# A drain at the end of each TensorE step in a graph-network layer, with the waits of the step's users moved to it

## The chip, the core and the metric

The kernel runs on one core of one Trainium2 chip. The metric is the device time of one execution in microseconds (us), the median of several runs. The engines are called as in the profile: PE (TensorE; PEld its weight loads), DVE (VectorE), ACT (ScalarE), POOL (GpSimd) and SP (SyncE). A "q" behind a name (PEq, PEldq, POOLq) means the engine's sequencer, the part that takes instructions from the queue, waits on semaphores and hands the work to the engine.

## The reference

One layer of a graph network, with 12,500 nodes of 64 numbers and 212,500 edges of 32 numbers. The edges come sorted by their destination. All data is float32.

```python
msg_in = jnp.concatenate([nodes[row], nodes[col], edge_features], axis=-1)
messages = relu(msg_in @ mW1 + mb1) @ mW2 + mb2
aggregated = jax.ops.segment_sum(messages, col, num_segments=12500)
upd_in = jnp.concatenate([nodes, aggregated], axis=-1)
out = layernorm(nodes + relu(upd_in @ uW1 + ub1) @ uW2 + ub2)
```

Here `row` is the source (`src`) and `col` the destination (`dst`) of each edge.

## The kernel before

The kernel has two branches; these inputs run `ordered`, which uses that the edges are sorted. The edges are cut into 554 groups (`G`) of three tiles of 128 edges; the last group has two tiles. All edges of a group go to at most 32 neighbouring nodes (a window, `W`), so that the node part of a message needs only 32 rows.

A group g passes through these parts:

- **gather(g)** (L129, L132): POOL starts three indirect DMAs, one a tile, that fetch the source nodes' rows into `own.s[g % 20]`. They wait for `turn_by[g - 20]`, the TensorE step that turned the group that had this buffer before. The loop calls `gather(k + 16)` after step k.
- **onehot(g)** (L303, L306): DVE writes the one-hot of each edge's destination in the window beside the gathered rows.
- **turn(g)** (L312): PE transposes the three tiles (L318) into PSUM, and ACT copies the result to `own.st` (L326), with a sum on the side that counts the edges of each node.
- **hidden(g)** (L334): six matmul records (three matmuls) give the hidden layer of the messages (L339), with the window's weights `own.wm`, and ACT applies relu (L349).
- **sums(g)** (L359): PE transposes the counts (L363), and three matmuls (six records, L365) add up the hidden rows of each destination. DVE adds the sums to `agg` (L374) and the counts to `xc` (L375).
- **windows(b)** (L288, L292): once in four groups a matmul makes the node part of the weights for the next four groups, and DVE copies it to `own.wm` (L297).
- **update** (L381): once a chunk of 512 nodes has all its edges, the node's own two-layer network, the residual and the layer norm follow, in pieces that `step_update` spreads over several steps. Its tiles (`u_ps`, `u`, `y` and so on) come from pools, and their waits are found from the tiles; they don't hang on the steps.

The order of the work is written out by hand. `step(*work)` (L445) issues the PE part of several parts, one behind the other, and then the ACT and DVE parts that use their results (`follow`). The waits are written by hand too: `after(first, *others)` lets one instruction wait for others. The first PE instruction of a step waits for everything that the step needs. Its other PE instructions wait for nothing, and only the last, `did[-1]`, raises PE's semaphore; the others are taken out of the semaphores by `no_tile_sem_insts`. That last instruction is given to each `follow`, which notes it in `turn_by`, `hidden_by` or `sums_by` and makes its ACT or DVE instruction wait for it. Gathers, one-hots and the loads of `own.st` wait for the steps in these notes as well.

In the main loop step k does turn(k), hidden(k-2) and sums(k-4) together. The PSUM buffers `own.ps` are two, taken in turn, so a step uses what ACT and DVE did for step k-2. The last ten values of k (`SHORT`) are split: a step with turn(k) alone, then up to two steps of sums, then up to two of hidden. `onehot(k + 1)` is called before step k.

## Time and profile before

| what | value |
|---|---|
| median of 3 runs | 2105.08 us (2103.44 to 2107.8) |
| profiled execution, its own time | 2103.22 us |
| its span, first to last instruction | 2101.4 us |
| mean granted clock of TensorE | 0.934 |
| PE busy | 1412.9 us (67%) |
| POOL busy | 1571.9 us (75%) |
| DVE, ACT busy | 575.0 us (27%), 553.4 us (26%) |
| PE 83 to 2049 us, busy | 1334.14 us of 1966 us |
| PE 2049 to 2096 us, busy | 37.03 us of 47 us |

A group row of the profile gives the line, the engine, the operation, what it writes and reads, the count, then the busy time in us and the mean of one in ns, and behind the second bar the time in which the engine sat idle just before these instructions and what ended most of it. In a timeline the columns are the start, the length, the engine, the line and the operation, and in brackets the idle time before it and what ended it. In the chain of waits the columns are start, length and what; "issue" is time in which the engine waited for nothing that the profile shows. In a row of one line or tile the three numbers are the least, median and greatest length in ns, then the first and last start. A releaser is inferred: it is the one that came last by the profile. The ends of matmuls are modelled.

### The profile page before, as it was taken

How to read it: one execution, taken by the hardware profiler on the slowest of the kernel's cores; microseconds unless marked ns; L12 is line 12 of the kernel's file. 1: busy time of each engine (PE TensorE's matmuls, PEld its weight loads, DVE VectorE, ACT ScalarE, POOL GpSimd, SP SyncE). 2: the span in 40 equal slices, each digit the busy share in tenths (PEclk: the TensorE clock that was granted, in tenths of full speed). 3: DMA queues.
4: the chain of work that ended last, by engine and by line, in shares of the span. 5: the costliest groups of instructions: out<-in, count | busy, mean ns of one | idle time of the engine just before them, and what ended most of it. 6: DMA issues, size and time to landing. Idle time of an engine off the chain costs nothing.

```text
span 2101.4 us, 30666 instructions
## 1 busy us (share of the span) xinstructions
PE 1412.9 (67%) x9441; PEld 1202.9 (57%) x9441; DVE 575.0 (27%) x3191; ACT 553.4 (26%) x1715; POOL 1571.9 (75%) x1668
## 2 busy tenths in 40 slices
PE   3766766666766767667666776776666766766667
PEld 2655655555655556556555665565555655655555
DVE  5322232222222223232222222222222223222222
ACT  1322222222222222222222222222222222222222
POOL 7777777777777777777777777777777777777774
PEclk9999999999999998999999999998999999999998
DMA  4321121221212112212121112121212121212211
GB/s 112 82 47 41 45 44 42 43 45 41 47 38 47 43 42 43 45 41 47 39 47 41 44 43 44 41 48 38 47 41 45 44 45 42 46 40 45 43 43 27
DMA packets 73364, 96.05 MB, mean 46 GB/s; under 512 B 33451, under 2 KB 40842, under 8 KB 73194
## 3 DMA queue, kind: packets, MB, share of 16 engines
q0 software_dynamic: 53152, 54.51, 13.8%
q1 hardware_dynamic: 19128, 39.03, 6.8%
q8 instruction: 80, 1.31, 0.3%
q14 instruction: 90, 0.74, 0.1%
q10 hardware_dynamic: 914, 0.46, 0.1%
HBM read 90.58 MB, written 3.20 MB: 45 GB/s over the span
## 4 chain that ended last, share of the span: by engine, by line
PE 40%; DMA 22%; issue 14%; POOL 12%; ACT 6%; DVE 5%; SPq 0%; POOLq 0%; ACTq 0%; DVEq 0%
DMA own_s<-in_x,src_sb 21%; PE own_ps L365 15%; POOL own_s L132 12%; PE own_ps L339 12%; PE own_ps L318 8%; ACT own_h L349 4%; ACT own_st L326 2%; PE own_ps L363 2%; DVE xc L375 1%; DVE own_s L306 1%; PE own_ps L292 1%; PE u_ps L405 1%; DVE agg L374 1%; PE u_ps L392 1%; PE u_ps L393 1%
## 5 line engine op out<-in xcount | busy, mean ns | idle before, releaser
L132 POOL DMA_INDIRECT own_s<-in_x,src_sb x1661 | 1571.1, 946 | 507.2 <-issue 355.3
L318 PE MATMUL own_ps<-own_ident,own_s 128*96 128x128 f32 x1661 | 300.2, 293 | 642.7 <-DVE own_s L306 250.9
L326 ACT ACTIVATE own_st<-own_ps 96x384 f32<-96x384 f32 x554 | 268.8, 485 | 1410.7 <-PE own_ps L365 1019.8
L318 PEld LDWEIGHTS own_ps<-own_ident,own_s 128*96 128x96 f32 x1661 | 171.6, 135 | 739.6 <-ACT own_h L349 691.1
L365 PE MATMUL own_ps<-own_s,own_h 128*128 128x128 f32 x3322 | 567.3, 312 | 0.0
L339 PE MATMUL own_ps<-own_wm,own_st 128*128 128x128 f32 x3322 | 502.7, 292 | 0.6 <-DVE own_wm L297 0.6
L374 DVE TENSOR_TENSOR agg<-own_ps,agg 128x32 f32 x554 | 106.0, 191 | 1397.9 <-ACT own_h L349 1369.0
L365 PEld LDWEIGHTS own_ps<-own_s,own_h 128*128 128x128 f32 x3322 | 454.7, 207 | 24.0
L339 PEld LDWEIGHTS own_ps<-own_wm,own_st 128*128 128x128 f32 x3322 | 455.6, 208 | 2.1 <-DVE own_wm L297 0.8
L349 ACT ACTIVATE own_h<-own_ps 128x384 f32<-128x384 f32 x553 | 262.3, 474 | 17.8 <-PE own_ps L339 17.8
L297 DVE COPY own_wm<-own_ps 32x128 f32<-32x128 f32 x550 | 155.1, 282 | 6.8 <-issue 0.8
L306 DVE TENSOR_TENSOR own_s<-iota,dlc 128x96 f32<-128x96 f32 x554 | 133.0, 241 | 4.3 <-issue 0.2
L363 PE MATMUL own_ps<-own_ident,own_counts 32*1 32x32 f32 x554 | 103.8, 187 | 3.8 <-ACT own_h L349 1.9
L326 ACT ACTIVATION_READ_ACCUMULATOR own_st<-own_ps 96x1 f32 x554 | 105.4, 190 | 0.0
L375 DVE TENSOR_TENSOR xc<-own_ps,xc 1x32 f32 x554 | 99.2, 179 | 14.7 <-PE u_ps L393 12.6
L363 PEld LDWEIGHTS own_ps<-own_ident,own_counts 32*1 32x1 f32 x554 | 41.1, 74 | 78.0 <-issue 13.6
L285 DVE COPY xw<-xc 66x32 f32 x554 | 62.6, 173 | 3.1 <-DMA xc<-in_xT 2.2
L292 PE MATMUL own_ps<-w1b,xw 66*128 66x128 f32 (+1 forms) x276 | 55.7, 284 | 0.0
L405 PE MATMUL u_ps<-u,u 128*128 128x64 f32 (+1 forms) x196 | 48.5, 391 | 0.5 <-ACT u L395 0.5
L405 PEld LDWEIGHTS u_ps<-u,u 128*128 128x128 f32 (+1 forms) x196 | 47.4, 326 | 1.0 <-ACT u L395 0.9
L292 PEld LDWEIGHTS own_ps<-w1b,xw 66*128 66x128 f32 (+1 forms) x276 | 44.2, 201 | 0.1
L407 DVE TENSOR_TENSOR y<-u_ps,xin 128x256 f32<-128x256 f32 (+1 forms) x25 | 10.5, 419 | 78.2 <-PE u_ps L405 78.2
(58 smaller groups left out, 203.6 us busy)
## 6 DMA issues: line engine op xcount, KB each, us to landing
own_s<-in_x,src_sb POOLq DMA_INDIRECT x1661, 2.4
own_st<-in_efT SPq DMA_DIRECT2D x138, 192.0 KB
xin<-in_x SPq DMA_DIRECT2D x24, 128.0 KB
out<-o SPq DMA_DIRECT2D x24, 128.0 KB
xc<-in_xT SPq DMA_DIRECT2D x12, 179.2 KB
dlc_i<-in_dst_cols SPq DMA_DIRECT2D x1, 831.0 KB
xc<-in_xT SPq DMA_DIRECT2D x4, 179.5 KB
src_sb<-in_src SPq DMA_DIRECT2D x13, 50.5 KB
```

Source lines behind the costliest of these rows:

```text
L132: nc.gpsimd.indirect_dma_start(out=s[:p, j, W:], out_offset=None, in_=x[:, :], in_offset=bass.IndirectOffsetOnAxis(ap=src_sb[:p, g * TG + ...
L292: did = nc.tensor.matmul(wp[: n * W, :], xw[:, :n, :], w1b, start=True, stop=True)
L297: c = nc.vector.tensor_copy(wm[g % NW][:W, :], wp[i * W : (i + 1) * W, :])
L306: places_by[g] = nc.vector.tensor_tensor(own.s[g % RING][:, :, :W], iota.unsqueeze(1).to_broadcast([P, TG, W]), dlc[:, g * TG : (g + 1) * ...
L318: nc.tensor.transpose(xt[:, j * P : j * P + p], s[:p, j, :], ident[:p, :p])
L326: nc.scalar.activation(t[: D + W, c : c + n], xt[:, :n], AF.Copy, accum_out=counts[:, g : g + 1]), step)
L339: nc.tensor.matmul(pre[:p, j, :], t[:, c + j * P : c + j * P + p], wm[g % NW], start=True, stop=True)
L349: relu_by[g] = [nc.scalar.activation(h, pre, AF.Relu)]
L363: did = [nc.tensor.transpose(sg[0:1, TIMES, :], counts[:W, g : g + 1], ident[:W, :W])]
L365: did.append(nc.tensor.matmul(sg[:, :TIMES, :], h[:p, j, :], s[:p, j, :W].unsqueeze(1).to_broadcast([p, TIMES, W]), start=j == 0, stop=j = ...
L374: after(nc.vector.tensor_tensor(agg[:, at], sg[:, 0, :], agg[:, at], ALU.add), step),
L375: after(nc.vector.tensor_tensor(xc[0:1, at], sg[0:1, TIMES, :], xc[0:1, at], ALU.add), step),
```

## The change

```diff
@@ -458,7 +458,8 @@
                 for b in [b for b in xws if (b - 1) * SB <= g][:1]:
                     last, copies = windows(b, own.ps[g % 2][:, 2, (TIMES + 1) * W :][:, :H])
                     did.append(last)
-        for i in did[:-1]:
+        did.append(nc.tensor.drain())
+        for i in did[:-2] if copies else did[:-1]:
             tc.no_tile_sem_insts.add(i.ins.name)
             tc.add_to_no_dep_group("quiet", i.ins)
         for part, g, _, _, follow in parts:
```

The pieces of `update` are issued after the step's last instruction, in the loop below the diff (`step_update(g)`), so they stand behind the drain on PE's queue.

## The prediction

> **What bounds the kernel now.** I read the costliest groups first, then the timeline of the gather queue, the chain of waits around one steady step and in the last 50 us, and last the rows by line. PE is busy longest of the compute engines (1412.9 us, 67%), but the row that matters is POOL's:

> ```profile
> L132 POOL DMA_INDIRECT own_s<-in_x,src_sb x1661 | 1571.1, 946 | 507.2 <-issue 355.3
> ```

> 1661 gathers of 946 ns, and most of the idle time before them is put down to "issue", which is no wait. The timeline of POOL, early, in the middle and at the end:

> ```profile
> 6.83 0.94 POOL L132 DMA_INDIRECT own_s<-in_x,src_sb  x1 [0.30 <-issue]
> 8.07 0.94 POOL L132 DMA_INDIRECT own_s<-in_x,src_sb  x1 [0.30 <-issue]
> ...
> 1008.27 0.94 POOL L132 DMA_INDIRECT own_s<-in_x,src_sb  x1 [0.30 <-issue]
> 1009.51 0.94 POOL L132 DMA_INDIRECT own_s<-in_x,src_sb  x1 [0.30 <-DMA own_s<-in_x,src_sb]
> ...
> 2078.95 0.90 POOL L132 DMA_INDIRECT own_s<-in_x,src_sb  x1 [0.30 <-issue]
> ```

> The pitch is 1.25 us throughout, with the same 0.30 us gap whether a releaser is named or not, and also at 7 us, before PE has begun its steps. So POOL never waits: 1661 x 1.25 = 2076 us of the 2101.4 us span, three gathers (3.75 us) a group. What PE waits for is seen in the chain of waits:

> ```profile
> 1008.27 2.50 DMA own_s<-in_x,src_sb
> 1010.77 0.14 issue
> 1010.91 0.51 PE own_ps L318 x3
> ```

> The third gather of a group starts at 1008.27, lands 2.50 us later, and PE's step starts 0.14 us after that. The next groups' third gathers, 1012.01 and 1015.75, give 1014.51 and 1018.25; the steps start at 1014.61 and 1018.43. The trace names a DVE instruction as releaser of those two, because it ended a moment before PE started. But the one-hot that step k needs is queued on DVE ahead of the adds of step k-1 (`onehot(k + 1)` stands before `step`), so it has been done for a step. A step's matmuls take about 2.15 us; in the windows view PE is busy 1334 us of the 1966 us between 83 and 2049 us. Over 1966 / 3.75 = 524 steps that leaves 1.2 us of idle PE a step, waiting for gathers.

> From 2049 us it is different. The last ten groups are split into separate steps, and the chain of waits runs through PE and ACT to the end without a gather in it:

> ```profile
> 2082.80 0.86 PE own_ps L365 x6
> 2083.66 0.68 PE own_ps L339 x6
> 2084.38 0.04 issue
> 2084.43 0.50 ACT own_h L349
> 2084.93 0.04 issue
> 2084.97 0.18 PE own_ps L363
> ```

> A sums step is followed at once by a hidden step, ACT's relu waits for that, the next sums step waits for the relu. Only here, in about 46 us, can a cost at the end of a step reach the end of the kernel.

> **The change part by part.**

> *In the steady part.* 580 drains are added to PE's queue, one a step (544 full steps, then 10 turns, 14 sums, 12 hiddens). Behind each stands the next step's first transpose, and in between its semaphore instructions. All of that lies in PE's 1.2 us of mean idle time, before the next gather has landed, so I cost it at nothing; without that cover it would cost y a step (below), 0.28 x 544 = 152 us. ACT and DVE get the step's end a little later, but step k needs only what they did for step k-2. POOL's gather for k+16 waits for the turn of step k-4, about 20 steps earlier: not late either. The loads on SP's queue wait for a hidden step nine steps before their use. At half clock a step's span grows to 3.73 us (2030.36 to 2034.09), just under POOL's 3.75; a drain puts PE some 0.3 us a step behind there, and it catches up at full clock. Early on (36 to 83 us) PE runs steps back to back, and the drains only stretch that stretch.

> *In the tail*, two prices. y: a step that starts behind another one's last matmul on PE. x: ACT or DVE waiting for a step's end. No row of this trace has a drain behind a busy array, so they are built from near rows:

> ```profile
> L365 PE MATMUL own_ps<-own_s,own_h x3322: 270/275/581, 44.9 to 2090.3; 128*128 128x128 f32 x196
> ...
> L318 PEldq EVENT_SEMAPHORE  x1243: 51/51/3273, 34.1 to 2085.4; - x178
> ...
> L826 PEldq DRAIN  x1: 8/8/8, 0.3 to 0.3; - x1
> ```

> A matmul lasts 0.275 us (median), but six take 0.86 us in the chain, a pitch of 0.143: each overlaps the one before by 0.13 us, and over a step's boundary that overlap goes. The drain itself is 0.008 us on an idle PE. I add 0.04 us for one hop, as "issue" shows between engines in the tail, and 2 x 0.051 us because the next weight load and matmul now come into the queue after the drain (the nearest row for an instruction on PE's sequencer is the 51 ns semaphore one). y = 0.13 + 0.008 + 0.04 + 0.10 = 0.28 us. x = 0.008 + 0.04 = 0.05 us, a second hop.

> Counting in the chain from 2049.04 on: PE goes from one step straight into the next work at 2051.75, 2053.47, inside the hidden pair after it, 2056.62, 2057.60, 2058.58, inside the next pair, 2066.54, 2068.90, 2073.34, 2079.03, 2080.75, 2083.66, 2086.02 and 2088.38, 15 times: 15 x 0.28 = 4.2 us. ACT or DVE takes over from a step's end 11 times (2049.56, 2055.47, 2060.00, 2062.37, 2064.87, 2067.22, 2081.99, 2084.34, 2086.70, 2088.94, 2090.53): 11 x 0.05 = 0.55 us. Besides, in five groups a turn stands between the hidden step and the sums step that waits for the relu. It had 0.30 us to spare (2084.67 to 2084.97). Now it starts y and two semaphore instructions (0.10) later and its own drain and restart (0.15) follow: 0.53 - 0.30 - 0.05 (x, already counted) = 0.18 us over, 5 x 0.18 = 0.9 us. Sum: 4.2 + 0.55 + 0.9 = 5.65 us.

> Bounds: the least is the drain row alone, 15 x 0.008 = 0.1 us. A gain is no end: the drain removes no work and cannot come before the matmul it follows. The most takes POOL's 0.30 us gap between two instructions as the restart: y = 0.43, 15 x 0.43 = 6.5 us, x = 0.15, 1.7 us, the turns 5 x 0.5 = 2.5 us, together 10.7 us. I take the middle, since its rows are PE's own.

> [...]

> **The rivals.**
> *The drain is nearly free.* The matmul's modelled end may lie after its real one, so the drain finds PE quiet at once and the restart hides under it: place, the same 15 crossings; price 0.05 us each, and no turn late: 15 x 0.05 + 0.55 = 1.3 us, 2106.4 us, no difference. It decides from y under about 0.2 us, where the sum falls below 0.2% (4.2 us, about what a measurement of this kernel can tell from no change). For it: the 8 ns row. Against: the 0.13 us overlap is real pitch, not a modelled end.
> *The steady part loses its cover.* If drain and restart took over the 1.2 us of idle, say 1.5 us, PE would be the bound: 0.3 x 544 = 163 us, about 2270 us. For it: no row bounds a drain under load. Against: every PE sequencer row here is 8 or 51 ns.
> *Faster.* Were the sequencer's semaphore earlier than the matmul's by the whole 0.04 us hop, 11 x 0.04 = 0.4 us comes back, 2104.7 us; only the spread of runs (2103.44 to 2107.8) would make more of it.

> **How the numbers follow.** The profiled execution took 2103.22 us (span 2101.4 and 1.8 around it); with the sum, 2108.9. The median of the runs is 1.9 us above the profiled one: 2105.08 + 5.65 = 2110.7 us, +0.27%. Chances: forecast 0.58, nearly free 0.34, lost cover 0.04, faster 0.04. Slower by over 0.2% is 0.58 + 0.04 = 0.62, within 0.34, faster 0.04. The range runs from 2105.0 (the 0.1 us bound) to 2117.0 (2105.08 + 10.7 and 1.2 us of spread); it leaves out the lost cover and the gains.

> **What would show it.** Right: POOL's pitch stays 1.25 us with the 0.30 us gap; steps still start 0.1 to 0.2 us after the third gather's landing; between 50 and 80 us plain steps that now start 1.98 us apart (58.71, 60.70, 62.67) start about 2.3 apart; POOL's last gather is still near 2079 us, and the time from it to the end, 22.5 us now, and from the first split step (2049) grow by 4 to 7 us. Wrong: a POOL pitch over 1.25 us, PE idle under 0.2 us in a steady step, or a granted clock well off 0.934, since a slower TensorE would leave its cover.

## The result and the profile after

The kernel with drains takes 2118.96 us (median of 4 runs, 2116.78 to 2124.34), the kernel before 2104.91 us beside it (4 runs, 2103.44 to 2107.8): a ratio of 1.0074 [1.0061, 1.0086], 14.05 us slower. I had forecast 5.65 us more and a range up to 2117.0. The profiled execution is the longest of the four, 2124.34 us with a span of 2122.5 us, so its tail shows the loss at its largest. Its granted clock is 0.910, where the kernel before has 0.934.

ACT's row in the kernel before:

```profile
L326 ACT ACTIVATE own_st<-own_ps 96x384 f32<-96x384 f32 x554 | 268.8, 485 | 1410.7 <-PE own_ps L365 1019.8
```

Three lines of after that answer to those of before, two groups of the page and the last gather in POOL's timeline:

```profile
L132 POOL DMA_INDIRECT own_s<-in_x,src_sb x1661 | 1572.5, 947 | 507.2 <-issue 370.6
L326 ACT ACTIVATE own_st<-own_ps 96x384 f32<-96x384 f32 x554 | 268.8, 485 | 1380.9 <-PEq L461 1329.8
...
2080.41 0.90 POOL L132 DMA_INDIRECT own_s<-in_x,src_sb  x1 [0.30 <-issue]
```

POOL is unchanged: 947 ns a gather, the same 507.2 us before them. ACT's wait now ends with PE's sequencer at line 461, the drain. The last gather starts 1.46 us later than before (2078.95). From there to the end of the span it takes 42.1 us, where it took 22.45. So 19.65 of the 21.1 us that this execution is longer show behind the last gather, in the split tail.

The row of the drain and one of its waiters, by line:

```profile
L461 PEldq DRAIN  x580: 438/2105/4497, 37.6 to 2110.7; - x194
...
  ACT own_st L326: 1329.8, 499
```

The 438 to 4497 ns contain the wait for the step's matmuls, so they are no price: in after's trace each of the 580 drains ends 0.02 to 0.05 us behind the modelled end of its step's last matmul, and the one of the step at 74.79, for example, starts at 74.86 and lasts 2.105 us, to 76.96. The price is in the gaps of PE. First the early phase, where steps run back to back (PE's timeline):

```profile
74.79 0.51 PE L318 MATMUL own_ps<-own_ident,own_s 128*96 128x128 f32 x3 [0.77 <-ACT own_st L326]
...
77.28 0.51 PE L318 MATMUL own_ps<-own_ident,own_s 128*96 128x128 f32 x3 [0.34 <-issue]
```

Plain steps are 2.49 us apart (1.98 before), with 0.34 us between the modelled end of the last matmul and the next transpose. Now the tail, in the chain of waits:

```profile
2078.03 0.08 issue
2078.11 1.65 PE own_ps L339 x6
2079.76 0.33 issue
2080.09 0.85 PE own_ps L318 x3
2080.94 0.08 issue
2081.02 0.21 PE own_ps L363
```

Into most hidden and sums steps PE loses 0.08 us behind the modelled end; into most turns, whose first instruction has two semaphore waits ahead of it, 0.34 us. Over all stops of after the least gap is 0.08 us with no semaphore instruction between the drain and the next matmul, 0.23 with one, 0.33 with two and 0.45 with three. Besides, the overlap with the matmul before is lost, 0.17 us at the end of a full step in before's timeline. Those are the stops I had priced. What I had not priced is the third column from the right of the windows view (span, busy time and instructions of PE, PEld, DVE, ACT and POOL, then TensorE's granted clock, DMA share, GB/s), first before, then after:

```profile
2050.00:2073.00 23.00, 19.99 (x129) 16.25 (x130) 6.72 (x36) 6.71 (x20) 17.28 (x19) 0.93 0.17 36
2073.00:2082.00 9.00, 7.63 (x34) 6.74 (x35) 4.29 (x22) 1.25 (x4) 5.32 (x6) 0.62 0.18 40
2082.00:2102.00 20.00, 8.91 (x58) 6.80 (x56) 3.34 (x18) 3.82 (x13) 0.00 (x0) 0.75 0.03 9
```

```profile
2050.00:2073.00 23.00, 19.15 (x79) 15.19 (x79) 5.04 (x27) 3.70 (x11) 17.21 (x20) 0.57 0.17 34
2073.00:2082.00 9.00, 8.01 (x32) 5.93 (x31) 1.30 (x7) 2.13 (x6) 6.49 (x7) 0.50 0.16 28
2082.00:2125.00 43.00, 26.23 (x114) 18.51 (x113) 8.55 (x45) 7.17 (x21) 0.00 (x0) 0.70 0.03 9
```

With drains TensorE runs at half clock from about 2053 to 2087 and from 2094 to 2104 us, 44 us in all; before it did so from 2051 to 2054 and from 2075 to 2082, 10 us, apart from the last few matmuls of each. The 1.65 us for six matmuls in the chain above is half clock too; at full clock it is 0.91.

### The profile page after: what moved, and what is told of

Same layout as the page of the kernel before. It is cut to its first block, busy times and chain, and to the rows that moved or that the text cites. A ratio compares the mean times of both kernels' runs of the same rounds, so it can differ in the third digit from the quotient of the medians.

```text
span 2122.5 us, 31419 instructions
## 1 busy us (share of the span) xinstructions
PE 1473.7 (69%) x9441; PEld 1238.3 (58%) x9441; DVE 574.5 (27%) x3191; ACT 554.1 (26%) x1715; POOL 1573.3 (74%) x1668
## 4 chain that ended last, share of the span: by engine, by line
DMA 32%; POOL 23%; PEldq 15%; issue 15%; PE 4%; ACT 4%; PEld 3%; DVE 3%; POOLq 0%; DVEq 0%; ACTq 0%
DMA own_s<-in_x,src_sb 32%; POOL own_s L132 23%; PEldq L461 15%; ACT own_st L326 2%; ACT own_h L349 2%; PEld own_ps L318 1%; PEld own_ps L365 1%; PE own_ps L365 1%; PE u_ps L405 1%; PEld own_ps L339 1%; DVE xc L375 1%; PE own_ps L339 1%; PE u_ps L392 1%; DVE agg L374 0%; PE u_ps L393 0%
## 5 line engine op out<-in xcount | busy, mean ns | idle before, releaser
L132 POOL DMA_INDIRECT own_s<-in_x,src_sb x1661 | 1572.5, 947 | 507.2 <-issue 370.6
L318 PE MATMUL own_ps<-own_ident,own_s 128*96 128x128 f32 x1661 | 301.7, 294 | 594.8 <-DVE own_s L306 163.1
L365 PE MATMUL own_ps<-own_s,own_h 128*128 128x128 f32 x3322 | 587.8, 320 | 0.0
L318 PEld LDWEIGHTS own_ps<-own_ident,own_s 128*96 128x96 f32 x1661 | 172.3, 135 | 700.3 <-ACT own_h L349 524.1
L339 PE MATMUL own_ps<-own_wm,own_st 128*128 128x128 f32 x3322 | 516.0, 297 | 1.1 <-issue 0.5
L365 PEld LDWEIGHTS own_ps<-own_s,own_h 128*128 128x128 f32 x3322 | 471.8, 214 | 24.7
L339 PEld LDWEIGHTS own_ps<-own_wm,own_st 128*128 128x128 f32 x3322 | 465.7, 212 | 5.5 <-issue 3.7
L349 ACT ACTIVATE own_h<-own_ps 128x384 f32<-128x384 f32 x553 | 262.4, 474 | 29.8 <-PEq L461 29.8
L363 PE MATMUL own_ps<-own_ident,own_counts 32*1 32x32 f32 x554 | 104.3, 188 | 3.0 <-ACT own_st L326 1.4
L363 PEld LDWEIGHTS own_ps<-own_ident,own_counts 32*1 32x1 f32 x554 | 41.1, 74 | 80.2 <-issue 20.4
L405 PE MATMUL u_ps<-u,u 128*128 128x64 f32 (+1 forms) x196 | 50.4, 400 | 2.6 <-ACT u L395 0.5
L405 PEld LDWEIGHTS u_ps<-u,u 128*128 128x128 f32 (+1 forms) x196 | 47.1, 324 | 7.4 <-issue 6.6
```

The costliest lines, as they stand in the source:

```text
L132: nc.gpsimd.indirect_dma_start(out=s[:p, j, W:], out_offset=None, in_=x[:, :], in_offset=bass.IndirectOffsetOnAxis(ap=src_sb[:p, g * TG + ...
L318: nc.tensor.transpose(xt[:, j * P : j * P + p], s[:p, j, :], ident[:p, :p])
L339: nc.tensor.matmul(pre[:p, j, :], t[:, c + j * P : c + j * P + p], wm[g % NW], start=True, stop=True)
L349: relu_by[g] = [nc.scalar.activation(h, pre, AF.Relu)]
L363: did = [nc.tensor.transpose(sg[0:1, TIMES, :], counts[:W, g : g + 1], ident[:W, :W])]
L365: did.append(nc.tensor.matmul(sg[:, :TIMES, :], h[:p, j, :], s[:p, j, :W].unsqueeze(1).to_broadcast([p, TIMES, W]), start=j == 0, stop=j = ...
```

## The experiments

My theory after the result, T1 in the texts on record: the loss is made of the stops in the split tail, as forecast, and of half clock that lasts longer there, because each stop leaves a hole in PE's work. T2 lays the loss on the main part, T3 on the semaphore that ACT and DVE wait for rather than on the stop of PE. Later rivals are told in the texts themselves. All edits are against the kernel after unless another one is named. Half clock in the main part is counted in slices of 1 us from 100 to 2040 us with a granted clock under 0.75; neighbouring slices make a stretch. Before: 53 stretches, 257 us, the longest 7 us. After: 45, 333 us, the longest 11 us. The runs fell on several chips; where nothing else is said, the kernel before took 2103.3 to 2104.9 us there, and times of different chips are set side by side on that ground.

### Where: tail or main part

`tail_only` has drains only in the 36 split steps, `steady_only` only in the 544 full ones (`not (...)` in place of the condition):

```diff
-        did.append(nc.tensor.drain())
-        for i in did[:-2] if copies else did[:-1]:
+        drained = work[0][1] >= G - SHORT or len(work) == 1 and work[0][0] is not turn
+        if drained:
+            did.append(nc.tensor.drain())
+        for i in did[:-2] if copies and drained else did[:-1]:
```

> Drains only at the steps of the split last ten groups (36 drains); the 544 full steps end as before. Theory T1: the whole loss (14 us) arises in the tail, about 6 us of it from stops at full clock and the rest because the gaps keep TensorE at half clock there; so 2114 to 2119 us, the last gather near 2079 us and some 36 to 40 us from it to the end (22.5 before). Rival T2: the 544 drains of the full steps put PE behind and the tail inherits it; then 2105 to 2111 us.

> Drains only at the 544 full steps, none in the split tail. T1: 2105 to 2107 us, since POOL's gathers cover them. T2: 2110 us or more. In both, the granted clock tells whether drains in the full steps lower it: after had 0.910 to 0.923, before 0.934.

Beside a kernel before of 2103.47 us, tail_only took 2124.92 us (2117.13 to 2128.11), 1.0089 [1.0069, 1.0109]; steady_only 2106.38 us, 1.0013 [1.0003, 1.0023]. The 36 drains of the tail make the whole loss; the 544 others cost about 2.9 us (0.6 to 4.8 by the interval). tail_only even took more than the kernel with all drains (2118.96 us) and than T1's 2114 to 2119: in its profiled execution, the longest, the tail was at half clock from 2052 us for 34 us and again from 2093 us to the end. So neither the early fall nor the long stay needs drains in the main part. In steady_only the last gather starts at 2081.84 us and the rest takes 22.2 us as before: its 2.9 us lie ahead of the tail, in POOL, whose gathers add up to 1573.9 us (1571.1 before). 61 of them follow the one before after 1.27 to 1.42 us instead of 1.25, where the kernel before has 24 of these. Why is open. The granted clock of its ten runs, 0.910 to 0.928, is below the 0.930 to 0.946 of the kernel before on that chip: the drains lower the clock in the main part too, but there it costs next to nothing. T2 falls.

### Which: the stop or the semaphore

`matmul_sem` keeps a drain at the end of each step, but the users wait for the last matmul as before:

```diff
-        did.append(nc.tensor.drain())
-        for i in did[:-2] if copies else did[:-1]:
+        for i in did[:-1]:
...
+        nc.tensor.drain()
```

> The drain stands at the end of every step, but ACT, DVE, POOL and SP wait for the step's last matmul as before. T1: the stop of PE's queue is what costs, so only the later wake of the users comes back, 11 handovers of about 0.1 us in the tail: 2117 to 2118 us. Rival T3: the wait on the sequencer's semaphore is what costs, and the stop is covered: 2105 to 2108 us.

2116.55 us (2109.37 to 2128.41), 1.008 [1.0051, 1.011], just under T1's range. The users are told as early as before (ACT's copy of a turn starts 0.04 us behind PE's modelled end, in after 0.12) and the loss is there all the same, so it is the stop of PE that costs, and T3 falls as the main cause. The spread of 19 us is itself a finding. The profiled run is the shortest, 2109.37 us; its tail saw half clock for only 10 us, and from its last gather it took 29.5 us, against 42.1 in after.

### The price of one stop

With gathers for the first 20 groups only (those of later groups are left out), POOL no longer sets the pace. `free_before` is that edit on the kernel before, `free_after` on the kernel after:

```diff
-        if k + AHEAD < G:
+        if k + AHEAD < RING:
             gather(...)
+        else:
+            loads[k + AHEAD] = []
```

> Gathers only for the first 20 groups; later groups reuse what those left, so PE, not POOL, sets the pace. Without drains. From 50 to 80 us of the kernel before, four steps took 9.5 us: 554 x 2.37 us and 50 to 60 us at both ends, 1370 to 1450 us, clock near 1.00.

> The same with the drains. From 50 to 80 us of the kernel after, four steps took 10.7 us: 554 x 2.67 us and the ends: 1530 to 1600 us at full clock, 0.3 us a step more than free_before. If the drains' holes alone bring half clock, up to 4.3 us a step and 2000 us or more, with a clock well under 1.00.

1463.79 and 1605.49 us, both a little over the ranges on record. The difference, 141.7 us over 554 groups, is 0.256 us a step on average, near the 0.3 expected. It is not the price of a bare stop: in about every fifth step PE waits for ACT or DVE anyway, 118 times for 144.6 us in all in free_before and 116 times for 102.6 us in free_after, and such a wait covers a stop in part. A transpose line from PE's timeline of each, at steps that follow at once, first free_before, then free_after:

```profile
1003.46 0.49 PE L318 MATMUL own_ps<-own_ident,own_s 128*96 128x128 f32 x3
```

```profile
1003.15 0.50 PE L318 MATMUL own_ps<-own_ident,own_s 128*96 128x128 f32 x3 [0.26 <-issue]
```

No gap in the one, 0.26 us in the other. From one turn to the next, with a matmul of `windows` in between, it is 2.20 us in free_before (1003.46 to 1005.66) and 2.64 us in free_after (1000.51 to 1003.15): 0.44 us for a stop that nothing covers. Both ran at a clock of 0.99 (0.993 and 0.990 in the profiled runs): stops in a row that is otherwise this dense did not bring TensorE down to half clock here.

### The clock: what it does in the main part

One stretch of half clock in each kernel, chosen because they begin alike (PE's timeline; before first, then after):

```profile
1865.32 0.85 PE L318 MATMUL own_ps<-own_ident,own_s 128*96 128x128 f32 x3 [0.91 <-DMA own_s<-in_x,src_sb]
...
1869.16 0.85 PE L318 MATMUL own_ps<-own_ident,own_s 128*96 128x128 f32 x3
1869.80 1.01 PE L339 MATMUL own_ps<-own_wm,own_st 128*128 128x128 f32 x6
```

```profile
1806.34 0.85 PE L318 MATMUL own_ps<-own_ident,own_s 128*96 128x128 f32 x3 [0.90 <-DMA own_s<-in_x,src_sb]
...
1810.52 0.85 PE L318 MATMUL own_ps<-own_ident,own_s 128*96 128x128 f32 x3 [0.34 <-issue]
1811.16 1.49 PE L339 MATMUL own_ps<-own_wm,own_st 128*128 128x128 f32 x6
```

Three transposes take 0.85 us at half clock, 0.50 at full. At half clock the step lasts 3.84 us in before (1865.32 to 1869.16) and 3.85 in after (1806.34 to 1810.19), against POOL's 3.75, and the next one does not wait for a gather. Before, it follows without a gap (1869.16), and in its middle the clock is back: 1.01 us for the six matmuls. After, a hole of 0.34 us stands there, and the whole next step passes at half clock (1.49 us) before it is back at about 1814. In these two that is the step from 7 us to 10. Over the whole main part, tail_only and tail_turn (below), which have no drains there, also stay at 7 us at most, as before.

In before and after a stretch lasts 3 to 4, 6 to 7 or 10 to 11 us. TensorE fell to half clock 53 times in the main part of the kernel before, and before the two falls shown PE's gaps were 1.5 to 1.7 us (1.52 and 1.63 in before, 1.47 and 1.70 in after).

`hole_prev`, made from the kernel before, has no drain. A full step's first PE instruction also waits for ACT's copy of the step before, which gives a hole of 0.67 us where steps run back to back:

```diff
-        after(did[0], *used, *(i for p in parts for i in p[3]))
+        k = work[0][1]
+        before_it = [copy_by[k - 1]] if len(work) > 1 else []
+        after(did[0], *used, *(i for p in parts for i in p[3]), *before_it)
```

`drain2` adds to the kernel after a second drain in each full step, ahead of its sums:

```diff
+            if part is sums and len(work) > 1:
+                nc.tensor.drain()
```

> No drains; in the main loop the first PE instruction of step k also waits for ACT's copy of step k-1, which opens a gap of 0.5 to 0.75 us between steps wherever they would run back to back, and none where PE waits for a gather anyway. The tail's steps are as before. T1 (the hole does it, the drain is only one way to make one): stretches at half clock in the main part last longer than the 7 us of before, clock 0.92 or less, 2104 to 2112 us. Rival T6 (the drain itself does it): stretches up to 7 us and a clock of 0.93 to 0.946 as before, 2103 to 2105 us.

> The changed kernel with a second drain in the middle of each full step, ahead of the sums. T1 (holes in a step keep TensorE at half clock once it is there): stretches at half clock longer than after's 10 to 11 us, a granted clock under 0.90, and, since a step at half clock then takes about 4.5 us against POOL's 3.75, 2125 us up to 2450 us if it never leaves it. Rival T5 (something else sets how long a stretch lasts): stretches of at most 11 us, and 2117 to 2124 us as after.

hole_prev: 2103.96 us, 0.9999 [0.9988, 1.0009]. Its main part has 38 stretches, 287 us; 16 of them last 10 us or more, the longest 17. In one of them (PE's timeline):

```profile
934.41 0.87 PE L318 MATMUL own_ps<-own_ident,own_s 128*96 128x128 f32 x3 [0.67 <-ACT own_st L326]
...
938.95 0.87 PE L318 MATMUL own_ps<-own_ident,own_s 128*96 128x128 f32 x3 [0.67 <-ACT own_st L326]
```

Hole after hole at 4.54 us a step, without a drain: holes alone prolong half clock. Here they cost no time, since POOL still sets the pace and PE has slack afterwards: the time fits T6, the stretches T1, and the clock of the eight runs (0.918 to 0.928) lies at the edge of T1's 0.92. drain2: 2114.96 us, 1.0051 [1.0031, 1.0071], with stretches up to 11 us as in after, so the longer ones that T1 expected did not come, and the time lies below both ranges on record. The second drain leaves a gap of only 0.08 to 0.1 us in the middle of a step. Holes of that size did not make the stretches longer than after's; how large one must be, these runs do not say.

### Keeping the clock up: fillers

`before_fill2` and `after_fill2` add two matmuls to each full step, whose result nobody reads:

```diff
+        if g < G - SHORT - 2:
+            did += [
+                nc.tensor.matmul(ps[:, 1, TG * H : (TG + 1) * H], t[:, c : c + P], wm[g % NW],
+                                 start=True, stop=True)
+                for _ in range(FILL)
+            ]
```

> The changed kernel with two more matmuls (four records, 0.57 us at full clock) in each full step, of which nobody uses the result; they lie in PE's idle time before the next gather. T1 with the clock: PE looks busier, the granted clock in the main part rises from 0.91 to 0.95 or more, the split tail starts at full clock, and the kernel gets faster although it does more: 2108 to 2114 us. Without the clock in it (the tail's stops alone cost 14 us): 2119 us or more, and the tail's length unchanged near 40 us.

> The kernel before with the same two idle-time matmuls in each full step, no drains. T1: the granted clock in the main part rises to about 0.99 as in after_fill2 and the tail starts at full clock; without drains it leaves half clock within 7 us if it falls, so 2101 to 2105 us, and 8 to 12 us less than after_fill2 (2114), which has the same main part. Rival T4 (the fillers themselves cost after_fill2 its time): 2108 us or more.

before_fill2 took 2101.24 us (10 runs, 2100.07 to 2102.45), 0.9991 [0.9981, 1.0]; after_fill2 2114.09 us (2109.64 to 2114.84), 1.0044 [1.0027, 1.0061]. In the main part half clock is all but gone: one stretch of 4 us, two of 3. In the last windows it is not, first after_fill2, then before_fill2:

```profile
2079.00:2112.00 33.00, 20.95 (x74) 15.08 (x74) 6.05 (x32) 5.42 (x17) 0.00 (x0) 0.50 0.04 11
```

```profile
2073.00:2082.00 9.00, 7.32 (x41) 6.30 (x41) 4.77 (x25) 2.20 (x7) 3.73 (x4) 0.64 0.15 37
2082.00:2100.00 18.00, 6.99 (x43) 5.16 (x42) 2.86 (x15) 2.87 (x10) 0.00 (x0) 0.71 0.03 8
```

Fillers stop where the split steps begin. Both kernels fall to half clock in the thin update matmuls of the tail (L405 of before, L412 here); the one without drains is out of it at 2079 us, the one with drains stays there for the last 33 us. So with the main part's clock mended, 12.9 us still lie between the two, in the medians and in the profiled spans, and of the latter 12.0 us lie behind the last gather. after_fill2 came to the upper end of T1's range although its split tail, which did start at full clock, fell to half clock after all. before_fill2 is also the only kernel here that may beat both: its interval ends at 1.0, and its last gather starts 2.15 us earlier, with 1568.9 us in POOL's gathers.

`before_short6_fill2` also sets `SHORT = 6` in it, `after_short4` sets `SHORT = 4` in the kernel after, to have fewer split steps.

> No drains: the two idle-time matmuls of before_fill2 (2101.2 us) and only six split groups instead of ten. If the split part enters at full clock and the shorter backlog suits it: 2098 to 2101 us. If splitting late leaves hidden steps behind at the end, as after_short4's chain showed: 2102 to 2108 us.

> The changed kernel with only the last four groups split (SHORT 4 instead of 10), so that six more groups run as full steps with one drain each, under the gathers. T1: the exposed stretch after the last covered step falls from about 50 us to about 25, and with it the chance to sit at half clock: 2104 to 2112 us, 8 us or more better than after (2119). T2 (main part): 2115 us or more.

2106.01 us, 1.0009 [0.9999, 1.0019], and 2122.39 us, 1.0082 [1.0065, 1.0099]: no gain. The first came out in the second of its two cases; the second was missed by over 10 us (it lies in T2's range, but steady_only had ruled T2 out). Now the update lands among the few split steps that are left (PE's timeline of after_short4):

```profile
2091.38 1.02 PE L365 MATMUL own_ps<-own_s,own_h 128*128 128x128 f32 x6
2094.15 3.37 PE L339 MATMUL own_ps<-own_wm,own_st 128*128 128x128 f32 x12 [1.74 <-DVE own_wm L297]
```

PE waits 1.74 us for DVE, and the 3.37 us for twelve matmuls are half clock, which holds from 2092 us on. This kernel changed more than the number of stops, so it tells little about them.

### Which drains of the tail

`tail_turn` has drains only at the ten turns of the tail, `tail_hidden` at its 12 hidden steps, `tail_sums` at its sums steps:

```diff
+        drained = work[0][1] >= G - SHORT and len(work) == 1 and work[0][0] is turn
```

Two windows in the text on tail_turn are two of the shortest stretches of half clock, of 3 to 4 us each: the 7 us at most that a stretch lasts in before's main part.

> Drains only at the ten turn steps of the split tail, where the sums step behind waits for ACT's relu anyway. T1: few stops on the chain and few holes, so half clock is left within two windows again: 2104 to 2109 us, against 2125 for 36 drains in the tail. Rival (any drain in the tail keeps half clock): 2114 us or more.

> Drains only at the twelve hidden steps of the split tail. The stop after a hidden step holds back the turn behind it, and with it the sums step, and ACT's relu comes some 0.1 us later: at full clock about 0.5 us a group, 4 to 5 us in all; if half clock also lasts, more: 2107 to 2113 us. Rival (the loss needs all 36 drains): 2105 us or less.

> Drains only at the sums steps of the split tail. Each stands between a sums step and the hidden step right behind it, on the chain, 0.2 us a time: 12 x 0.2 = 2.4 us at full clock, 2105 to 2108 us; with half clock kept by them 2109 us or more.

tail_turn took 2103.86 us beside 2103.88, 1.0 [0.999, 1.001]. In its timeline the sums step behind a drained turn waits for ACT's relu anyway:

```profile
2085.79 0.18 PE L363 MATMUL own_ps<-own_ident,own_counts 32*1 32x32 f32 x1 [0.31 <-ACT own_h L349]
```

The stop lies inside a wait that was there before (it had 0.30 us to spare). The two others ran on a chip on which the kernel before itself took 2525.74 us and POOL waited. There they cost 1.0016 [1.0007, 1.0026] and 1.0022 [1.0012, 1.0033], 4.7 and 5.2 us (at full clock 4 to 5 and 2.4 had been expected): each is a piece of the loss, but the chip's other bound makes the sizes unfit for the sum. There the main part, which has no drains in these two, also had stretches of half clock of up to 11 and 14 us, so the 7 us hold only where POOL sets the pace.

### Stops without half clock

The pair with fillers once more, and with the update of the last full chunk left out, in whose matmuls the tail fell to half clock:

```diff
-    waiting = [(closes, update(base, p, n)) for base, p, n, closes in PLAN]
+    waiting = [(closes, update(base, p, n)) for base, p, n, closes in [*PLAN[:-2], PLAN[-1]]]
```

> before_fill2 without the update of the last full chunk of 512 nodes (those rows of the output are left out), whose thin matmuls and vector work bring TensorE to half clock near 2075 us in the middle of the split tail. No drains. 2095 to 2101 us; the tail at full clock.

> after_fill2 without the same update. With the update, after_fill2 and before_fill2 stand 12.9 us apart (2114.1 and 2101.2). T1 (half clock that the drains keep up is part of the loss): the tail stays at full clock, so only the stops are left and the two stand 6 to 9 us apart. Rival (the stops alone make the loss, the clock is a bystander): still 11 to 14 us apart.

This first try fell on the chip just named: 2547.03 us, 1.009 [1.0073, 1.0107], and 2611.33 us, 1.0345 [1.0327, 1.0363]. It does not answer the question, but 64 us between the two show something else, here in POOL's timeline of the second:

```profile
1007.27 0.94 POOL L133 DMA_INDIRECT own_s<-in_x,src_sb  x1 [1.82 <-PEq L468]
...
1011.87 0.94 POOL L133 DMA_INDIRECT own_s<-in_x,src_sb  x1 [1.16 <-PEq L468]
```

The gathers wait for PE's drains. There POOL does not set the pace, and the main part's drains are not covered. That is the place of the prediction's second rival, but not its mechanism: PE does not become the bound there, it still waits 520.3 us for gathers. The same two kernels on another chip:

> As fill2_noupd_before (before_fill2 without the update of the last full chunk, whose output rows are left out), on another chip: the run before fell on a chip where all kernels, the unchanged one too, took some 420 us longer and POOL itself waited. 2095 to 2101 us here, the tail at full clock after about 2055.

> As fill2_noupd_after. T1 (half clock that the drains keep up is part of the loss): the tail stays at full clock, and the two stand 6 to 9 us apart instead of 12.9. Rival (the stops alone make the loss): 11 to 14 us apart.

noupd_before2 took 2096.21 us (5 runs, 2095.41 to 2096.94), 0.9963 [0.9949, 0.9977]; noupd_after2 2102.96 us (10 runs, 2100.8 to 2123.28), 1.0018 [0.9991, 1.0046]. The turns of the tail, at full clock (PE's timeline, first noupd_before2, then noupd_after2):

```profile
2065.30 0.50 PE L319 MATMUL own_ps<-own_ident,own_s 128*96 128x128 f32 x3
2067.66 0.49 PE L319 MATMUL own_ps<-own_ident,own_s 128*96 128x128 f32 x3
```

```profile
2078.59 0.51 PE L319 MATMUL own_ps<-own_ident,own_s 128*96 128x128 f32 x3 [0.34 <-issue]
2081.57 0.50 PE L319 MATMUL own_ps<-own_ident,own_s 128*96 128x128 f32 x3 [0.34 <-DMA own_s<-in_x,src_sb]
```

A group takes 2.36 us without drains and 2.98 with. The medians are 6.75 us apart, the spans of the two profiled runs 6.0: that is the price of the stops with hardly any half clock added (in their tails 9 us of it without drains and 13 with). It is rather too low for the kernel with its update: at its last three turns noupd_before2 waits for gathers again (0.33, 1.54 and 0.21 us), which covers a part of the stops. Of noupd_after2's ten runs, seven took 2100.8 to 2104.15 us at a clock of 0.992 to 0.996, and three 2113.9, 2122.19 and 2123.28 us at 0.988, 0.983 and 0.981. So the same kernel takes some 12 to 21 us more when its clock is lower, and the five runs without drains do not scatter.

## Why the prediction was right and wrong

**Right: what bounds, and where.** POOL's pitch stayed at 1.25 us, the full steps' drains stayed under the wait for gathers (steady_only), and the loss came behind the last gather (tail_only). The two signs named for the steps themselves came out: plain steps of the early phase 2.49 us apart, 0.51 more (about 0.3 foreseen), and the last gather near 2079 us (2080.41). The third did not: the time from the last gather to the end was to grow by 4 to 7 us and grew by 19.65 in the profiled execution.

**The stops: right in kind and nearly in size.** The sum of y, x and the late turns was 5.65 us; the pair without the update gives 6.75 and 6.0, and in the profiled matmul_sem, whose tail saw half clock no longer than before's, the time behind the last gather grew by 7.0. The terms were off in both directions. In the noupd pair a group grew by 0.62 us, and its parts can be read from the starts of the steps. From sums to hidden 0.24 us were added, under my y of 0.28. From hidden to the next turn 0.60 were added (0.67 to 1.27): two semaphore instructions stand there, and I had one price for all crossings. From the turn to the next sums step 0.22 were saved out of the 0.30 to spare. I had 0.51 for such a group (0.28 + 0.18 + 0.05). The timeline of before has six groups with a turn in that place, not the five that I counted. x was 0.05; ACT's relu starts 0.12 to 0.14 us after the modelled end where it took 0.09 to 0.10, so it is 0.02 to 0.04, and 0.08 for the copy of a turn. The turn's own stop, 0.15 us in the sum, measured nothing alone (tail_turn), since it fits into the 0.30; a turn is late only once the hidden step ahead has stopped too.

**Wrong: the clock had no term.** The step that failed is the tail's sum itself. It priced stops at the durations of before's tail, that is, at before's clock there, and named the clock only as a sign at the very end ("a granted clock well off 0.934, since a slower TensorE would leave its cover"). That looked for the harm in the main part; it came in the tail, where no gather wait gives the time back. In the profiled tail a group takes 4.8 us from turn to turn at half clock (2095.02 to 2099.82 us) and 3.0 at full; before, 3.64 (2078.16 to 2081.80) and 2.36. An estimate from these rows: 44 us of half clock are 9.2 groups at 1.8 us more each, 16.5 us; before's 10 us are 2.7 groups at 1.28, 3.5 us; the difference is 13.0 us, and with the stops' 6.75 it makes 19.8. The time from the last gather to the end grew by 19.65. That the two come so close is in part luck, since half clock also fell on other work than these groups. The three long runs of noupd_after2 bear the price out: by their clocks they have 26, 47 and 56 us more of half clock than the other seven, which at 1.8 us in 4.8 makes 10, 18 and 21 us (an estimate); they are 12, 20 and 21 us longer. In the median of 14.05 us about half is stops and half is clock, if the 6.75 us hold for this kernel too.

**What is shown and what is not.** Shown: that the tail's stops make the loss (tail_only, steady_only), that it is PE's stop and not the user's semaphore (matmul_sem), that holes without drains prolong half clock (hole_prev), that the tail can keep half clock for over 30 us with drains and did not without, and that with little half clock about 6 to 7 us remain (the last pair). For the tail the profiled runs say this together: in seven whose tail has no drains, or only those at its turns (before, steady_only, tail_turn, hole_prev and the three filler kernels without drains), no stretch lasts over 10 us; of those with drains at every step of the tail, after, tail_only, drain2, after_fill2 and after_short4 have stretches of 31 to 34 us, while matmul_sem and noupd_after2 have none over 10 us, in executions that were among the shorter ones of their kernels. So drains make a long stay likely, not certain. Only argued: that half clock in the tail prolongs itself through the same holes as in the main part. No kernel with a dense tail and drains was made. Open: why one execution falls to half clock at the start of the tail (before at 2051 us too, for 3 us, after at 2053 and tail_only at 2052 for 34 us) and another does not (matmul_sem), how large a hole must be, and why some gathers come later when PE is late.

**The rivals.** Nearly free (2106.4) fell on the 0.34 us into turns and on the clock; a drain on an idle PE takes 8 ns, as that rival said, but in the tail PE is not idle. The lost cover did not come where POOL sets the pace (steady_only); on the chip where POOL waits the main part's drains did cost time, but by another way than that rival's. Nothing was faster: the users' earlier wake-up did not come, they woke later. The price of a drain was 0.44 to 0.51 us a step where full steps run back to back (free_after, the early phase of after).

## What to carry to other kernels

Price a stop by its place: nothing where a longer wait follows anyway (tail_turn 1.0 [0.999, 1.001]), 0.2 to 0.6 us where PE's steps run back to back (0.24 and 0.60 in the noupd pair's tails, 0.44 in free_after, 0.51 in after's early phase), more the more semaphore instructions the next step begins with (0.08 us with none to 0.45 with three in after). Then ask what the hole does to the granted clock. With holes between its steps TensorE stayed at half clock longer here (stretches of up to 17 us in hole_prev against 7 in before), so a stage that is on the critical path can lose as much again, and a sum made from the durations of before must also be made once at half clock. Where PE idled under POOL, a few matmuls that nobody reads kept the clock at 0.99 (0.994 in before_fill2, 0.934 in before); without drains that made little of the time (0.9991 [0.9981, 1.0]), since PE was not the bound.

## What the runs showed of the hardware

In the main part of before, in which PE is busy about two thirds (1319 of 1940 us), TensorE fell to half clock 53 times, 257 us in all; PE's gaps ahead of the two falls shown, one of before and one of after, were 1.5 to 1.7 us. Two more matmuls in every step all but ended that (4 us in before_fill2). free_after, dense but for 0.26 us a step and a wait of about 0.9 us in every fifth, ran at 0.99. In after, a matmul behind a drain starts 0.08 us or more after the modelled end of the one before, and each semaphore instruction in between adds 0.10 to 0.15 us (0.08, 0.23, 0.33 and 0.45). A chip was met on which the unchanged kernel took 2525.74 us, 20% more; in the kernels profiled there POOL's gathers are broken by waits, and nothing here says why.
